# Output projection in 49 products of 128 columns instead of 28 of 256, in a post-norm transformer block on one NeuronCore

## The chip, the cores and the metric

The kernel runs on one core of one Trainium2 chip. The core has a matrix engine (TensorE, "PE"), a vector engine (VectorE, "DVE"), a scalar engine (ScalarE, "ACT"), a general engine (GpSimd, "POOL") and a queue engine (SyncE, "SP") that issues transfers. Each engine takes its instructions in one fixed order, and an instruction waits until what it needs has been signalled by other engines. The metric is the device time of one execution in microseconds (us).

## The reference

Input `x` is 2 sequences (b) of 512 tokens with 512 features, all in float32. The block has two halves:

```
q, k, v = x @ Wq.T, x @ Wk.T, x @ Wv.T        # 32 query heads, 8 key/value heads, 128 wide
q, k    = rmsnorm(q) * qw, rmsnorm(k) * kw
attn    = softmax(q k^T / sqrt(128) + alibi, causal)
x       = layernorm(x + (attn @ v) @ Wo.T)
x       = layernorm(x + ((silu(x @ gate.T * gs) * (x @ up.T * us)) @ down.T) * ds)
```

One group g has one key/value head and its 4 query heads. What the change is about is the output projection `(attn @ v) @ Wo.T`: per group and sequence, 512 tokens by 512 inner features (4 heads of 128) by 512 output features, summed over the 8 groups.

## The kernel before

Work is cut into units (g, b, i): a group, a sequence and a tile of 128 tokens; two neighbouring tiles make a pair. For each pair the kernel projects q, k and v (`project`), normalises and turns them (`heads`), computes scores and softmax tile by tile (`scores`), turns the probabilities and multiplies by v (`attend`), and multiplies the result `aT` by the group's part of Wo (`project_out`). Groups 0 to 5 run over both sequences one after the other; groups 6 and 7 are ordered by sequence, so that the feed-forward half of sequence 0 can start before the attention of sequence 1 is over. Then come the feed-forward part (`ffn_weights`, `ffn_up`, `ffn_down`) and the second normalisation.

**Seven products in place of eight.** The three large matrix products (q/k/v, output, feed-forward) treat their factors as 2 by 2 blocks and form 7 block products in place of 8, by Winograd's form of Strassen's scheme. `seven` (line 619) issues them by the table `PLAN`; the products of sums need four sums of blocks of each factor, which `sums_a` and `sums_b` compute with `tensor` (line 571) on DVE or POOL. For the output projection one product is `depth` = 2 matmuls of 128 by 128 by 256: two token tiles make the rows, two heads each the inner blocks, 256 output features the columns. After each product `accumulate` adds the accumulator bank into `y`, the residual held in the core's memory.

**How a matmul shows.** In float32 one matmul of the program is two records in the trace, each with its own load of weights (LDWEIGHTS) and its own pass over the columns; a transpose is one record. So the 448 output matmuls (8 groups x 2 sequences x 2 pairs x 14) show as 896 records of 128x256 at line 628.

**What sets the order.** All work is entered as operations with a cost, a priority and dependencies, and a planner in `emit` (line 168) places them in time by these costs, chooses DVE, POOL or ACT where several can do an operation, and emits each engine's instructions in the planned order. Buffers come from rings with a number of slots (`Ring`); an operation that needs a slot is planned after the slot's last user. Accumulator banks come from the ring `f` (3 banks) for the large products. Memory is divided into stages: buffers of q/k/v and attention are closed when their last user is placed, and buffers of the feed-forward part open in their place (`close`).

Loads go through SP's queue in planned order; at the start, ACT's queue carries some of them. `load_qkv` loads the group's q, k and v weights from three tensors, `load_o` the group's part of Wo (1 MB), `load_x` the turned input.

Of the kernel before, what the change touches and what calls it, by code (L numbers as in the profile page):

```python
# [10 lines left out]
F32 = mybir.dt.float32  # L11
# [6 lines left out]
P = 128  # L18
# [11 lines left out]
Q = 32  # L30
# [8 lines left out]
MAX_INIT = 3e38  # L39
EARLY = 4  # L40
# [34 lines left out]
class Ring:  # L75

    def __init__(self, name, bufs, shape, dtype=F32, gate=None):
        self.name, self.bufs, self.shape, self.dtype = name, bufs, shape, dtype
        self.gate = gate  # L80
        self.pool = None
        self.slots = [None] * bufs

    def room(self):

        best = None
        for k, b in enumerate(self.slots):
            t = 0.0
            for u in b.users if b else ():
                if u["end"] is None:  # L90
                    break
                t = max(t, u["end"] + LAG[u["eng"]])
            else:
                if best is None or t < best[0]:
                    best = (t, k)
        return best

    def take(self, b):
        k = self.room()[1]
        self.slots[k] = b  # L100
        b.tile = self.pool.tile(self.shape, self.dtype, tag=f"{self.name}{k}", name=b.name, bufs=1)
# [14 lines left out]
class Work:  # L116
# [51 lines left out]
    def emit(self):  # L168
# [23 lines left out]
        def room(o):  # L192

            t = o["at"]
            for b in o["takes"]:
                if b.tile is not None:
                    continue
                r = b.ring
                if r.gate is not None and r.gate["end"] is None:
                    return None  # L200
                found = r.room()
                if found is None:
                    return None
                t = max(t, found[0])
            return t
# [56 lines left out]
def post_ln_block(  # L262
# [4 lines left out]
    wqt: bass.AP,  # L267
    wkt: bass.AP,
    wvt: bass.AP,
# [30 lines left out]
    def ring(stage, name, bufs, shape, dtype=F32, gate=None):  # L300
        r = Ring(name, bufs, shape, dtype, gate)
# [11 lines left out]
    r_y = ring("all", "y", 1, [P, NT, DM])  # L313
    r_xT = ring("all", "xT", 2, [P, NK, S])
    r_sx = ring("all", "sx", 2, [P, 4, 2, S // 2])
    r_gs = ring("all", "gs", 1, [P, NF])
    r_us = ring("all", "us", 1, [P, NF])
    r_ds = ring("all", "ds", 1, [P, DM])
# [4 lines left out]
    r_ms = ring("all", "ms", 3, [P, 2, G + 1])  # L323
    r_inv = ring("all", "inv", 3, [P, 2, G + 1])
# [3 lines left out]
    r_stats = ring("all", "stats", 3, [P, 2, 6])  # L328
# [5 lines left out]
    r_tq = ring("qkv", "tq", 1, [P, 4, 2, W3])  # L334
    r_c = ring("qkv", "c", 2, [P, 2, 2, W3])
    r_sq = ring("qkv", "sq", 2, [P, 2, G + 1, HD])

    r_wo = ring("att", "wo", 2, [P, G, DM])
    r_to = ring("att", "to", 1, [P, 4, 2, WO])
    r_kT = ring("att", "kT", 2, [P, S])  # L340
    r_v = ring("att", "v", 2, [P, NTB, HD])
    r_qT = ring("att", "qT", 6, [P, NQ, G, Q])
    r_bias = ring("att", "bias", 2, [P, S])
    r_prT = ring("att", "prT", 5, [P, S])
    r_aT = ring("att", "aT", 3, [P, 2, G, P])
    r_so = ring("att", "so", 1, [P, 4, 2, P])
    r_rel = ring("att", "rel", 1, [P, S])
    r_vs = ring("att", "vs", 3, [P, HD])
# [8 lines left out]
    y = fixed(r_y, "y")  # L357
    gs_sb, us_sb, ds_sb = fixed(r_gs, "gs_sb"), fixed(r_us, "us_sb"), fixed(r_ds, "ds_sb")
    qw, kw = fixed(r_qw, "qw"), fixed(r_kw, "kw")
    ident, nhalf, rel = fixed(r_id, "ident"), fixed(r_nh, "nhalf"), fixed(r_rel, "rel")  # L360
# [12 lines left out]
    first_pair = {}  # L373
    for p, (g, b, i) in enumerate(pairs):
        first_pair.setdefault(g, p)
# [9 lines left out]
    def load_qkv(g, prio):  # L385
        w = Buf(r_w, f"w_{g}")
        w_qkv[g] = w
        src = wqt[:, ts(g, G * HD)].rearrange("(kc p) (n c) -> p kc n c", p=P, n=2)
        for kc in range(NK):
            at = prio + 0.01 * kc  # L390

            def queries(ns, kc=kc, at=at, queue="SP"):
                load(
                    0.13 * len(ns),
                    at,
                    lambda q: q.dma_start(
                        w[:, kc, ns[0] : ns[-1] + 1, : 2 * HD], src[:, kc, ns[0] : ns[-1] + 1]
                    ),
                    [(w, ("q", n, kc)) for n in ns],
                    queue=queue,  # L400
                )

            def other(n, kc=kc, at=at, queue="ACTQ"):
                load(
                    0.066,
                    at + 0.001,
                    lambda q: q.dma_start(
                        w[:, kc, n, 2 * HD :], (wkt, wvt)[n][ts(kc, P), ts(g, HD)]
                    ),
                    [(w, ("kv", n, kc))],  # L410
                    queue=queue,
                )

            if g == 0 and kc == 0:

                queries((0,))
                load_x(0, kc, 0, at, "ACTQ", 2)
                other(0, queue="SP")
                queries((1,), queue="ACTQ")
                other(1, queue="SP")  # L420
            else:
                queries((0, 1))
                if g == 0:
                    load_x(0, kc, 0, at, "ACTQ")
                    other(0)
                    other(1)
        if g > 0:
            for n, other in enumerate((wkt, wvt)):
                load(
                    0.26,  # L430
                    prio + 0.05,
                    lambda q, n=n, other=other: q.dma_start(
                        w[:, :, n, 2 * HD :],
                        other[:, ts(g, HD)].rearrange("(kc p) c -> p kc c", p=P),
                    ),
                    [(w, ("kv", n, kc)) for kc in range(NK)],
                )

    def load_x(b, kc, q, prio, queue="SP", parts=1):

        n = NTH // parts
        for k in range(parts):
            c0 = q * NTH + k * n
            load(
                0.13 / parts,
                prio + 0.0001 * k,
                lambda e, c0=c0: e.dma_start(
                    xT[b][:, kc, c0 : c0 + n], xt[ts(kc, P), b * S + c0 : b * S + c0 + n]
                ),
                [(xT[b], (kc, c0 // P + m)) for m in range(n // P)],  # L450
# [6 lines left out]
    def w_keys(g, kcs, ns=(0, 1)):  # L457
        w = w_qkv[g]
        return [(w, (k, n, kc)) for k in ("q", "kv") for kc in kcs for n in ns]

    def load_o(g, prio):
        wo = Buf(r_wo, f"wo_{g}")
        w_o[g] = wo
        load(
            1.05,
            prio,
            lambda q: q.dma_start(wo.tile, wot[ts(g, G * HD), :].rearrange("(h p) c -> p h c", p=P)),
            [A(wo)],
        )
# [26 lines left out]
    for b, q in ((0, 1), (1, 0), (1, 1)):  # L496
        for kc in range(NK):
            load_x(b, kc, q, -8.6 + 0.05 * (2 * b + q))
    load_o(0, -8.4)
    load(  # L500
        2.1,
        -8.3,
        lambda q: q.dma_start(y.tile, x.rearrange("(t p) c -> p t c", p=P)),
        [(y, (t, n)) for t in range(NT) for n in range(2)],
    )
# [37 lines left out]
    def make_bias(g, prio):  # L543
        bg = Buf(r_bias, f"bias_{g}")
        bias[g] = bg
        for h in range(G):
# [4 lines left out]
                    bg[ts(h, Q), :], rel[ts(h, Q), :], SLOPES[g * G + h], 1.0, ALU.mult, ALU.mult  # L551
                ),
                [(rel, h)],
# [29 lines left out]
    def sums_a(n, prio, s, a, s_key, a_keys, **kw):  # L583

        add, sub = ALU.add, ALU.subtract
# [3 lines left out]
        tensor(n, prio, g(0), f(1, 0), f(1, 1), add, k(1, 0) + k(1, 1), [s_key(0)], **kw)  # L589
        tensor(n, prio, g(2), f(0, 0), f(1, 0), sub, k(0, 0) + k(1, 0), [s_key(2)], **kw)  # L590
        tensor(n, prio, g(1), g(0), f(0, 0), sub, [s_key(0)] + k(0, 0), [s_key(1)], **kw)
        tensor(n, prio, g(3), f(0, 1), g(1), sub, k(0, 1) + [s_key(1)], [s_key(3)], **kw)

    def sums_b(n, prio, t, b, t_key, b_keys, **kw):

# [1092 lines left out]
```

## Time and profile before

| | |
|---|---|
| median of 3 runs | 1053.89 us (1053.85 to 1054.01) |
| profiled execution, its own time | 1054.3 us |
| its span, first to last instruction | 1052.3 us |
| PE busy | 1043.9 us, 99% |
| DVE, ACT, POOL busy | 633.8, 422.8, 490.0 us |
| granted PE clock | 0.999 |
| PE starts its first real matmul at | 4.39 us |
| last PE record begins at about | 1046 us |

The ends of PE records are modelled: a record of 256 columns is listed with 379 ns although the next one starts some 216 ns later. So the price of a record is read from the distance of starts in the timeline, and not from its listed duration.

### The profile page before, as it was taken

The page shows a single profiled execution, that of the slowest core. Times are in us where ns is not written, and L with a number is a line of the kernel's source. Part 1 is how long each engine was busy: PE and PEld are TensorE (multiplying, and loading weights), DVE is VectorE, ACT ScalarE, POOL GpSimd, SP SyncE. Part 2 cuts the span into 40 slices and gives each one's busy share as a digit, 9 for nine tenths or more (in the row PEclk, how much of TensorE's full clock was granted, in tenths as well). Part 3 has the DMA queues.
Part 4 walks back from the last instruction along what each step waited for, and adds up shares of the span by engine and source line. Part 5 has one row for each costly group of instructions (what it writes and reads, how often), then busy time and mean ns, then how long its engine had stood idle before and what let it go on. Part 6 is the DMA issues. An engine that isn't in the chain of part 4 may idle for free.

```text
span 1052.3 us, 13348 instructions
## 1 busy us (share of the span) xinstructions
PE 1043.9 (99%) x4610; PEld 764.6 (73%) x4610; DVE 633.8 (60%) x1599; ACT 422.8 (40%) x1047; POOL 490.0 (47%) x666
## 2 busy tenths in 40 slices
PE   9999999999999999999999999999999999999997
PEld 5676767676767676767676767676767788888886
DVE  6755565556655565556555656565676477667544
ACT  2543434443434344434444444444454523434100
POOL 6873545454444544454445545454574342114230
PEclk9999999999999999999999999999999999999999
DMA  8310012001100120012001200100101012230011
GB/s 252 119 60 1 1 41 61 1 1 41 60 1 1 40 61 1 1 40 62 1 1 40 61 1 1 40 1 1 40 1 41 21 41 80 76 88 21 1 40 40
DMA packets 44450, 38.93 MB, mean 37 GB/s; under 512 B 3712, under 2 KB 36864, under 8 KB 44384
## 3 DMA queue, kind: packets, MB, share of 16 engines
q1 hardware_dynamic: 42512, 36.92, 11.4%
q10 hardware_dynamic: 1872, 1.18, 0.4%
q8 instruction: 36, 0.59, 0.2%
q14 instruction: 30, 0.25, 0.1%
HBM read 35.99 MB, written 2.10 MB: 36 GB/s over the span
## 4 chain that ended last, share of the span: by engine, by line
PE 99%; DMA 1%; DVE 0%; POOLq 0%; issue 0%; ACT 0%; DVEq 0%
PE pa_q L628 15%; PE sc L958 12%; PE pa L1066 11%; PE pa_o L628 11%; PE pb_q L628 8%; PE pa_h L628 7%; PE pt L1047 6%; PE pb_o L628 5%; PE pc_q L628 4%; PE pb_h L628 4%; PE pa_d L628 3%; PE ptq L905 3%; PE pc_o L628 3%; PE pc_h L628 2%; PE pb_d L628 2%; PE px L1101 2%
## 5 line engine op out<-in xcount | busy, mean ns | idle before, releaser
L983 ACT ACTIVATE pr<-pr,nmax 128x32 f32<-128x32 f32 (+15 forms) x256 | 132.4, 517 | 99.9 <-DVE nmax L967 97.7
L958 PE MATMUL sc<-kT,qT 128*128 128x160 f32 (+15 forms) x512 | 147.9, 403 | 0.0
L1015 POOL TENSOR_SCALAR pr<-pr,rden 128x64 f32<-128x64 f32 (+12 forms) x288 | 135.2, 489 | 12.8 <-DVE rden L998 12.4
L1066 PE MATMUL pa<-prT,v 128*128 128x512 f32 (+1 forms) x320 | 137.0, 510 | 0.0
L967 DVE CUSTOM_DVE_ANT_0 pr<-sc,bias 128x32 f32<-128x32 f32 (+15 forms) x256 | 110.3, 439 | 42.1 <-PE sc L958 39.6
L958 PEld LDWEIGHTS sc<-kT,qT 128*128 128x128 f32 x512 | 88.7, 190 | 53.6 <-issue 29.8
L576 DVE TENSOR_TENSOR y<-y,pa_o 128x256 f32<-128x256 f32 x128 | 53.7, 419 | 95.8 <-PE pa_o L628 95.1
L705 ACT COPY c<-pa_q 128x384 f32<-128x384 f32 x90 | 42.9, 478 | 141.1 <-PE pa_q L628 139.8
L628 PE MATMUL pa_q<-tq,sx 128*128 128x384 f32 x248 | 90.3, 487 | 0.1
L1047 PEld LDWEIGHTS pt<-ident,pr 128*128 128x128 f32 x576 | 69.4, 141 | 28.9 <-issue 15.5
L562 POOL TENSOR_TENSOR inv<-ms,nhalf 128x10 f32<-128x10 f32 (+1 forms) x33 | 63.3, 1919 | 54.9 <-DVE ms L849 53.7
L1047 PE MATMUL pt<-ident,pr 128*128 128x128 f32 x576 | 81.7, 273 | 0.1
L705 ACT COPY prT<-pt 128x512 f32<-128x512 f32 (+1 forms) x92 | 50.3, 549 | 59.2 <-PE pt L1047 59.0
L827 ACT ACTIVATE sq<-c 128x640 f32<-128x640 f32 x64 | 47.2, 738 | 57.7 <-DVE c L576 57.2
L707 DVE COPY prT<-pt 128x512 f32<-128x512 f32 (+1 forms) x68 | 42.1, 627 | 42.7 <-PE pt L1047 42.7
L576 POOL TENSOR_TENSOR sq<-c,inv 128x640 f32<-128x640 f32 x54 | 67.2, 1256 | 0.7
L628 PE MATMUL pa_o<-to,so 128*128 128x256 f32 x256 | 65.7, 379 | 0.0
L707 POOL COPY v<-c 128x128 f32<-128x128 f32 x36 | 10.8, 299 | 116.1 <-DVE c L576 110.5
L1066 PEld LDWEIGHTS pa<-prT,v 128*128 128x128 f32 x320 | 53.4, 191 | 15.1 <-issue 0.5
L576 POOL TENSOR_TENSOR so<-aT 128x256 f32<-128x256 f32 x32 | 22.9, 727 | 87.8 <-PE pb_o L628 72.3
L628 PEld LDWEIGHTS pa_q<-tq,sx 128*128 128x128 f32 x248 | 45.3, 190 | 25.4 <-issue 7.2
L912 ACT ACTIVATE qT<-ptq,qw 128x512 f32<-128x512 f32 x61 | 41.9, 687 | 51.6 <-PE ptq L905 50.8
(161 smaller groups left out, 2085.5 us busy)
## 6 DMA issues: line engine op xcount, KB each, us to landing
wo<-in_wot_dram SPq DMA_DIRECT2D x8, 1024.0 KB, 5.6
w<-in_wqt_dram SPq DMA_DIRECT2D x31, 256.0 KB, 4.1
wi<-in_gwt_dram SPq DMA_DIRECT2D x14, 256.0 KB, 2.8
wi<-in_uwt_dram SPq DMA_DIRECT2D x14, 256.0 KB, 3.2
wdi<-in_dwt_dram SPq DMA_DIRECT2D x10, 256.0 KB, 3.3
y<-in_x_dram SPq DMA_DIRECT2D x1, 2048.0 KB, 12.9
w<-in_wkt_dram SPq DMA_DIRECT2D x7, 256.0 KB, 4.9
w<-in_wvt_dram SPq DMA_DIRECT2D x7, 256.0 KB, 5.2
```

Source lines behind the costliest of these rows:

```text
L562: lambda e: nc.gpsimd.tensor_tensor(dst(), src(), nhalf[:, :n], ALU.pow),
L576: lambda e: vec[e].tensor_tensor(dst(), a(), b(), alu),
L628: nc.tensor.matmul(bank[:rows, :width], lhsT=a(fa, c), rhs=b(fb, c), start=(fresh and c == 0), stop=(c == depth - 1), skip_group_check=True,)
L705: nc.scalar.copy(dst(), src())
L707: vec[e].tensor_copy(dst(), src())
L827: lambda e, r=r: nc.scalar.activation(sq[:, r].rearrange("p h d -> p (h d)"), c(r)[:, : 5 * HD], AF.Square),
L958: lambda e, a=a, w=w, sc=sc: nc.tensor.matmul(sc[:, :w], lhsT=qT[:, a, :, :], rhs=kT[:, :w], start=True, stop=True),
L967: lambda e, a=a, w=w, sc=sc: nc.vector.tensor_tensor_reduce(out=pr[:, a, :w], in0=sc[:, :w], in1=bg[:, S - w :], scale=-1.0, scalar=MAX_IN ...
L983: lambda e, a=a, w=w: nc.scalar.activation(pr[:, a, :w], pr[:, a, :w], AF.Exp, bias=nmax[:, a : a + 1], scale=-1.0, accum_out=den[:, a : a ...
L1015: lambda e, a=a, c0=c0, n=n, to=to, c1=c1: nc.gpsimd.tensor_scalar(to[:, a, c1 : c1 + n], pr[:, a, c0 : c0 + n], rden[:, a : a + 1], 1.0, ...
L1047: nc.tensor.transpose(pt[:, ts(k, P)], pr[:, a, ts(j, P)], ident.tile)
L1066: lambda e, j=j, prT=prT, n=n: nc.tensor.matmul(po[:, S - n :], lhsT=v[:, j, :], rhs=prT[:, :n], start=(j == 0), stop=(j == i), skip_group ...
```

## The change

For groups 0 to 5 (`DEEP` = 6) the output projection of a whole sequence of a group is done at once, with the scheme of seven products at two levels: the outer one on blocks of 256 tokens x 256 inner x 256 output features, the inner one on 128 x 128 x 128. That makes 49 matmuls of 128 by 128 by 128 per group and sequence, where there were 28 of 128 by 128 by 256. The outer products are done in two rounds (four, then three of them); within a round the same inner product of each outer one lies side by side in a bank, so one addition of 128x512 (or 128x384) on DVE takes it away. The sums of outer products are not made in every group: the seven outer products have a cell each in `acc` (two of 7 x 2 x 256 columns), in which they add up over the six groups. Three cells have no place in `y` and start from zero; the four others start as the residual, so that `acc` replaces `y`. After group 5, `gather` combines the seven cells to the four of `y` (14 additions of 128x256 per sequence). Groups 6 and 7 keep one level of seven products, pair by pair (`project_pair`).

More changes come with it:

- `sums_a` and `sums_b` write the first of the four sums over a block that nothing needs afterwards, so rings of sums have 3 slots of a sum instead of 4. Product 5 now uses those blocks. Because weights are overwritten, groups 6 and 7 load their weights once per sequence instead of once.
- Rings change their sizes: `qT` 6 to 3, `sq` 2 to 1, `wo` 2 to 1, `ms`, `inv` and `stats` 3 to 2; in the feed-forward part `wi`, `wf`, `sw` and `gu` from 2 to 1 with a second slot that opens when attention's memory is closed. `vs` goes from 3 to 4.
- The ALiBi bias of a group is made from the bias of the group before, by a ratio of slopes, and the table `rel` has a slot of the bias ring.
- Inputs are laid out with longer rows per transfer: q, k and v weights of a group lie together (rows of 1.5 or 3 KB, one tensor in place of three), `xt` loads four feature chunks in one transfer after the first ones, `wo` and `x` are loaded with rows of 8 and 4 KB. The load of `ds` moves from the start to the feed-forward part.

```diff
-    def project_out(p, prio):
-        g, b, i = pairs[p]
...
-        done, _ = accumulate(t, prio)
-        seven(prio, Factor(a_ap, a_keys), Factor(b_ap, b_keys), P, WO, 2, f"o{p}", done)
+    ROUNDS = (
+        [(2, ("A", 3), ("B", 3)), (4, ("A", 1), ("T", 3)), (1, ("A", 2), ("B", 1)), (5, ("A", 0), ("B", 0))],
+        [(6, ("S", 1), ("T", 1)), (3, ("S", 3), ("B", 2)), (7, ("S", 2), ("T", 2))],
+    )
+    def project_out(g, b, prio):
...
+        sums_a(
+            4 * P,
+            prio,
+            lambda j: so[:, j - 1],
+            lambda r, k: heads_of(1 - r, k),
+            lambda j: (so, j),
+            lambda r, k: keys_of(1 - r),
+        )
+        for number, outer in enumerate(ROUNDS):
+            n = len(outer)
+            si = Buf(r_si, f"si_{g}_{b}_{number}")
...
+            def done(which, bank, c0=c0, n=n):
+                r, k = INTO[which]
...
+                tensor(
+                    n * P,
+                    prio,
+                    cell,
+                    cell,
+                    lambda: bank[:, : n * P].rearrange("p (m c) -> p m c", m=n),
+                    ALU.add,
+                    [A(bank)] + keys,
+                    keys,
+                    ("DVE",),
+                )
+            inner(prio, Factor(a_ap, a_keys), Factor(b_ap, b_keys), n, f"o{g}_{b}_{number}", done)
+    def inner(prio, a, b, n, name, done):
+        banks = {k: Buf(r_f, f"p{k}_{name}") for k in "abc"}
+        last = ()
+        for which, k, fa, fb, fresh in PLAN:
+            bank = banks[k]
+            def mm(e, bank=bank, fa=fa, fb=fb, fresh=fresh):
+                for c in range(n):
+                    nc.tensor.matmul(
+                        bank[:, ts(c, P)],
+                        lhsT=a(fa, c),
+                        rhs=b(fb, c),
+                        start=fresh and c == 0,
+                        stop=True,
+                        skip_group_check=True,
+                    )
...
+            W.add({"PE": n * 0.22}, prio, mm, reads, [A(bank)], last if fresh else ())
...
+            done(which, bank)
+    def gather(b, prio):
+        for r in range(2):
+            for to, what in ((2, 1), (6, 1), (3, 6), (3, 5), (7, 6), (4, 7), (7, 5)):
...
     def sums_o(g, prio, after):
...
+        if g >= DEEP:
+            return
+        ti = t_i[g] = Buf(r_ti, f"ti_{g}")
+        for src, c0, keys in ((w, 0, [(w, m) for m in range(4)]), (t, 4, [(t, j) for j in (1, 2, 3)])):
+            n = len(keys)
+            sums_b(
+                n * P,
+                prio,
+                lambda j, c0=c0, n=n: ti[:, j - 1, c0 : c0 + n, :],
+                lambda r, n, src=src: src[:, :, r, ts(n, P)],
+                lambda j, c0=c0: (ti, (j, c0)),
+                lambda r, n, keys=keys: keys,
+                after=after,
+            )
...
-    r_qT = ring("att", "qT", 6, [P, NQ, G, Q])
+    r_qT = ring("att", "qT", 3, [P, NQ, G, Q])
...
-    r_wi = ring("up", "wi", 2, [P, 2, NK, P], I32, gate_up)
-    r_wf = ring("up", "wf", 2, [P, 2, NK, P], F32, gate_up)
+    r_wi = ring("up", "wi", 1, [P, 2, NK, P], I32)
+    r_wf = ring("up", "wf", 1, [P, 2, NK, P])
...
+    for r in (r_wi, r_wf, r_sw, r_gu):
+        r.add(ring("down", r.name + "b", 1, r.shape, r.dtype))
```

## The prediction

> **What bounds the kernel now.** First the page's busy times and the chain of work that ended last:
>
> ```profile
> PE 1043.9 (99%) x4610; PEld 764.6 (73%) x4610; DVE 633.8 (60%) x1599; ACT 422.8 (40%) x1047; POOL 490.0 (47%) x666
> ...
> PE 99%; DMA 1%; DVE 0%; POOLq 0%; issue 0%; ACT 0%; DVEq 0%
> ```
>
> PE is busy throughout and is the whole chain. A busy PE may still be held up inside, so I next read the waits of PE by what they waited for. All of them:
>
> ```profile
> PE warm L482 <- POOL ident masks.py:199: 1.3, 1, 1.3
> PE pa_h L628 <- ACT gu L705: 0.5, 1, 0.5
> PE pa_q L628 <- DVE c L707: 0.4, 1, 0.4
> PE pp L724 <- DMA w<-in_wkt_dram: 0.2, 1, 0.2
> ```
>
> That is 2.4 us in 1052. So the time is the number of PE records times the price of each; other engines count only where they make PE wait. The price comes from the timeline of PE, from distances of starts (columns: start, duration, engine, line, operation, count):
>
> ```profile
> 500.61 1.03 PE L628 MATMUL pa_o<-to,so 128*128 128x256 f32 x4
> 501.47 1.03 PE L628 MATMUL pb_o<-to,so 128*128 128x256 f32 x4
> 502.33 1.03 PE L628 MATMUL pa_o<-to,so 128*128 128x256 f32 x4
> 503.19 1.04 PE L1047 MATMUL pt<-ident,pr 128*128 128x128 f32 x8
> 504.07 1.03 PE L628 MATMUL pa_o<-to,aT 128*128 128x256 f32 x4
> ```
>
> Four records of 256 columns take 0.86 us, 0.216 each, whether a product or something else follows. Eight transposes of 128 columns take 0.88, about 0.109 each. Half the columns, half the price, if that holds for a matmul.
>
> **The change: the product records.** It is not certain that it holds: a matmul also loads 128x128 float32 weights, and the listed load of a matmul (190 ns) is longer than that of a transpose (141 ns), as the page's groups say. The only 128-column matmuls before are among the scores of the first tiles. Here is PE with its weight loads in the timeline:
>
> ```profile
> 532.31 0.55 PE L958 MATMUL sc<-kT,qT 128*128 128x32 f32 x4
> 532.31 0.41 PEld L958 LDWEIGHTS sc<-kT,qT 128*128 128x128 f32 x3 [0.24 <-issue]
> ...
> 532.65 0.30 PEld L1066 LDWEIGHTS pa<-prT,v 128*128 128x128 f32 x2
> ...
> 533.62 0.61 PE L958 MATMUL sc<-kT,qT 128*128 128x96 f32 x4
> 533.62 0.41 PEld L958 LDWEIGHTS sc<-kT,qT 128*128 128x128 f32 x3 [0.24 <-issue]
> 533.95 0.30 PEld L1066 LDWEIGHTS pa<-prT,v 128*128 128x128 f32 x2
> 534.06 0.59 PE L1066 MATMUL pa<-prT,v 128*128 128x512 f32 x1
> ```
>
> At 532.31 the matmuls have only 32 and 64 columns, so the weight loads set the pace: three starts of loads span 532.31 to 532.65, 0.113 each. At 533.62 (96 and 128 columns) it is 0.11. A load of matmul weights thus takes about 0.112 us and can run beside the matmul before it, and it is slightly longer than the 0.109 of the columns. I take 0.112 per record; it is the nearest row. The bounds are 0.109 (the transposes' pace) and 0.120 (a little is lost at every change of product).
>
> A rule speaks against this. The Trainium skill, page "TensorE: Matmul & The Clock Gate", section "Back-to-back issue gap", says that in a stream of weight loads and matmuls both set the spacing, and gives 81 ns for 128 columns where the columns alone would take 56: 1.45 times. An estimate by that factor: 0.109 x 1.45 = 0.158 us per record, and the new projection would cost 186 us in place of 145. The rows above have precisely such a pair stream at 0.110 to 0.113, in float32; the row decides, and the rule stays as a rival.
>
> Now the count. Before, groups 0 to 5 have 6 x 2 x 2 pairs x 14 matmuls x 2 records = 672 records at 0.216: 145.2 us. After: 6 x 2 x 49 x 2 = 1176 records at 0.112: 131.7 us. **Saved: 13.5 us** (17.0 at 0.109, 4.1 at 0.120). Groups 6 and 7, q/k/v, attention and feed-forward keep their PE records. All this lies on the path, since PE is the path.
>
> **What is added beside PE.** On DVE, 168 additions of a bank of 256 columns at 0.419 (70.4 us) become 84 of 512 columns and 84 of 384. Rows of the same kind of addition from a bank:
>
> ```profile
> L576 DVE TENSOR_TENSOR y<-y,pa_o 128x256 f32<-128x256 f32 x128 | 53.7, 419 | 95.8 <-PE pa_o L628 95.1
> ...
> L576 DVE TENSOR_TENSOR c<-pb_q,c 128x384 f32<-128x384 f32 x62 | 34.4, 554 | 32.7 <-PE pb_q L628 32.6
> ...
> L576 DVE TENSOR_TENSOR y<-y,ps 128x512 f32<-128x512 f32 x8 | 5.5, 685 | 0.9 <-PE ps L1593 0.9
> ```
>
> 84 x 0.685 + 84 x 0.554 = 104 us, so 34 us more. Sums of the left factor were 8 x 256 columns per group and sequence and are now 4 x 512 (outer), 8 x 256 and 4 x 384 (inner): 3,584 more columns, 43,000 over twelve. Inner sums of weights add 4 x 512 + 4 x 384 per group, 21,500. The gathering adds 28 x 256, 7,200. Together 71,700 columns of two-operand work: 96 us if all on DVE (0.685 per 512), 178 us if all on POOL (1.271 per 512, the row of `to` from `wo`). In the built kernel's instruction lists they are mixed, and some old work moves from POOL to DVE; costing every changed row by the durations of its kind, DVE gains 81 us and POOL 60, ACT 22. That makes DVE about 715 us (69%), POOL 550 (53%), ACT 445: all still covered by PE's 1030 us. Fill of `acc` with zeros (3,072 columns, some 2.8 us of DVE before 9 us) lies under the wait for the first weights: DVE idles 2.2 us there now.
>
> **Where a wait could come on PE.** PE's order is fixed, so I looked in it for the distance between a result and its use, counting PE work by the paces above. The first inner product of a round waits for the sums; for round one these can begin when the last part of `aT` is added. From the end of that last attention matmul (`pz`) to the first inner product there lie 10 to 25 us of other PE work in all twelve cases. The chain needs two sums of 512 and four of 256 columns: 2 x 0.685 + 4 x 0.44 = 3.1 us on DVE, 2 x 1.27 + 4 x 0.73 = 5.5 us on POOL. Round two needs the single `si` slot back and four sums of 384: 2.4 to 4 us, against 3.5 to 8 us of other PE work. Tighter is the bank: a product is added away before the next goes on top of it. That addition is 0.27 us longer than now, and the order leaves 0.5 us or more of other work after it. What stands in front on DVE can use this up: the queue behind a late addition holds score maxima, evictions of transposes and so on, all of which PE waits for in turn. Two-operand sums also stretch when both engines work (POOL's `tq` sums have 2577 ns in one group, 1814 in another, same size). Smaller rings (`qT`, `sq`, and the feed-forward's single slots around 840 us) are planned for in the same way. I put **+1.5 us** on all this; 0 to +10 bounds it, since before, the same kind of order lost 0.9 us after the start.
>
> **The start.** The plain first projection is 32 records at 0.323 = 10.3 us, and took 11.5 us (4.39 to 15.89), so late loads cost 1.2. Fewer, longer first transfers can gain at most that; PE cannot begin before 4.39, since its warm-up ends there. Against it: the third product (`pb_q`) now needs sums written over weights and input that the plain products still read, made by POOL at 1.81 a sum after the projection; before, PE waited about 0.3 us at this place. I count 0, with -1.2 to +2. `ds` moves out of the start and to a place with no traffic: nothing. Loads in between are shorter in number and covered by tens of us; `wo` with one slot loads in 5.6 us and has 35 us or more between its last use and the next. The end, 6 us after the last PE record, is unchanged.
>
> **Sum.** Against the profiled execution: 1054.3 - 13.5 + 1.5 + 0 = 1042.3. The median shown is 0.4 lower than that execution, so 1053.9 - 12.0 = **1042 us**.
>
> **Rivals.**
> 1. Full pace: matmuls of 128 columns run at 0.109 as transposes do, nothing waits, the start gains its 1.2: 1053.9 - 17.0 - 1.0 = 1036 us. For it: the difference is 3 ns per record. Against: the loads at 532 us.
> 2. Half eaten: PE waits for additions and sums in many rounds, say 0.3 us in each of 24 rounds; with 0.114 per record (-11) it gives 1053.9 - 11 + 7 = 1050 us. For it: DVE at 69%, more sharing. Against: 2.4 us of waits now, at 60%.
> 3. Slower: DVE's additions become the pace within a round. There a round has 7 products of 0.67 or 0.9 us, one addition each of 0.55 or 0.69. From 13.5 / 168 = 0.08 us per product on, waits outweigh the saving; at 0.15 us per product (25 us) it ends at 1066. Against: each round is mixed with other PE work.
> 4. The spacing rule: 186 - 145 = +41, 1095 us. Against: the rows.
> That the change does not do what it says is excluded for PE's counts: the built instruction list has 588 matmuls of 128x128 and 112 of 128x256 for the output, in place of 448.
>
> **Chances.** Forecast 0.70 (1038 to 1047), rival 1 0.12, rival 2 0.10, rival 3 0.06, rival 4 0.02. A difference under 0.2% (2.1 us) can hardly be told from none; that takes 0.03 out of rival 2. Faster 0.89, same 0.03, slower 0.08. For the range I leave out rivals 3 and 4 and the outer end of the first: 1036 to 1050.
>
> **What would show it.** The records `pa_o` of 128x128 should start 0.112 apart inside a product (right), or 0.109, or 0.12 and more (that step wrong). PE's busy time should fall to about 1032, PE's waits stay under 5 us in all; waits on DVE `acc` additions or on `si` above 10 us would make the forecast wrong, as would a late start of the third product by more than 2 us. DVE should show 700 to 730 us.

## The result and the profile after

The changed kernel takes 1043.28 us (median; 1043.01 to 1043.42), the kernel before beside it 1053.87 us (1053.72 to 1054.01). The ratio is 0.9899 with an interval of 0.9887 to 0.9911: 10.6 us faster. The forecast was 1042.0, with 1036 to 1050 as its range. The profiled execution took 1043.3 us, its span is 1041.5 us, and the granted clock is 0.999 as before.

The page of the changed kernel, busy times and the chain of work that ended last:

```profile
PE 1031.9 (99%) x5114; PEld 768.8 (74%) x5114; DVE 719.0 (69%) x1669; ACT 433.7 (42%) x1097; POOL 567.6 (54%) x724
...
PE 97%; DVE 1%; DMA 1%; POOL 0%; issue 0%; ACT 0%; ACTq 0%; POOLq 0%; DVEq 0%
```

PE has 504 more records (5114 for 4610) and is busy 12.0 us less. It is still the chain, but no longer quite alone in it: 3% of the chain lie on other engines, where it was 1%. The waits of PE by what they waited for (total us, times, longest us):

```profile
PE warm L458 <- POOL ident masks.py:199: 1.3, 1, 1.3
PE pb_q L607 <- DVE c L548: 0.6, 1, 0.6
PE pa_o L607 <- ACT aT L704: 0.5, 1, 0.5
PE pp L723 <- DMA xT<-in_xt_dram: 0.4, 1, 0.4
PE ptq L910 <- DVE sq L548: 0.4, 1, 0.4
PE ptk L932 <- DVE sq L548: 0.3, 1, 0.3
PE pa_q L607 <- ACT c L704: 0.2, 1, 0.2
```

They make 3.7 us, 1.3 more than before. None waits for an addition into `acc`, nor for the sums `si` of the inner products. The price of a record, again from distances of starts in PE's timeline:

```profile
137.11 1.06 PE L1300 MATMUL pa_o<-ti,si 128*128 128x128 f32 x8
138.00 0.60 PE L1052 MATMUL pt<-ident,pr 128*128 128x128 f32 x4
138.44 1.02 PE L1071 MATMUL pa<-prT,v 128*128 128x512 f32 x2
```

Eight records of 128 columns take 0.89 us (137.11 to 138.00), 0.111 each; the four transposes behind them take 0.44, 0.110 each. Over all 1176 records of the two-level projection the mean distance is 0.112 us and the sum 131.7 us, against 145.1 before. The additions on DVE, each shape on its own:

```profile
L548 DVE TENSOR_TENSOR acc<-acc,pa_o 128x512 f32<-128x512 f32 x48 | 32.9, 686 | 17.8 <-PE pa_o L1300 17.1
L548 DVE TENSOR_TENSOR acc<-acc,pa_o 128x384 f32<-128x384 f32 x48 | 26.6, 553 | 23.1 <-PE pa_o L1300 21.8
```

DVE waits for PE before them, and not PE for DVE. From all distances of starts, PE's records add up to 1044.9 us before and 1034.0 after. The 10.9 us between them are 13.4 gained in the projection less 2.5 given back in small delays. The list of waits shows about half of these (its 1.3). Most of them lie at 150 to 200 us (0.9) and at 750 to 850 us (1.6). At 181 us the timeline shows what PE waited for:

```profile
178.80 1.80 POOL L548 TENSOR_TENSOR tq<-w,tq 128x768 f32<-128x768 f32 x1
179.11 2.91 DVE L548 TENSOR_TENSOR sq<-c,inv 128x640 f32<-128x640 f32 x2
```

The first of the two DVE operations ends at 181.29. It took 2.18 us, where the 34 of its kind have a median of 0.82, and POOL's sum stood beside it; `ptq` on PE started at 181.43, 0.57 us later than its pace (0.4 of this is in the list).

### The profile page after: what moved, and what is told of

Its sections match the earlier page's. It is cut to its first block, busy times and chain, and to the rows that moved or that the text cites. A ratio compares the mean times of both kernels' runs of the same rounds, so it can differ in the third digit from the quotient of the medians.

```text
span 1041.5 us, 14505 instructions
## 1 busy us (share of the span) xinstructions
PE 1031.9 (99%) x5114; PEld 768.8 (74%) x5114; DVE 719.0 (69%) x1669; ACT 433.7 (42%) x1097; POOL 567.6 (54%) x724
## 4 chain that ended last, share of the span: by engine, by line
PE 97%; DVE 1%; DMA 1%; POOL 0%; issue 0%; ACT 0%; ACTq 0%; POOLq 0%; DVEq 0%
PE pa_q L607 15%; PE sc L963 12%; PE pa L1071 11%; PE pa_h L607 7%; PE pb_q L607 7%; PE pa_o L1300 7%; PE pt L1052 6%; PE pc_q L607 4%; PE pb_h L607 4%; PE pb_o L1300 4%; PE pa_d L607 3%; PE ptq L910 3%; PE pa_o L607 3%; PE pc_h L607 2%; PE pc_o L1300 2%; PE pb_d L607 2%
## 5 line engine op out<-in xcount | busy, mean ns | idle before, releaser
L1020 POOL TENSOR_SCALAR pr<-pr,rden 128x64 f32<-128x64 f32 (+12 forms) x288 | 151.1, 541 | 39.6 <-DVE rden L1003 36.5
L963 PEld LDWEIGHTS sc<-kT,qT 128*128 128x128 f32 x512 | 86.3, 190 | 40.6 <-issue 17.0
L548 DVE TENSOR_TENSOR acc<-acc,pa_o 128x512 f32<-128x512 f32 (+2 forms) x128 | 72.9, 570 | 57.1 <-PE pa_o L1300 38.9
L704 ACT COPY prT<-pt 128x512 f32<-128x512 f32 (+1 forms) x123 | 65.8, 541 | 96.1 <-PE pt L1052 94.7
L704 ACT COPY gu<-pa_h 128x256 f32<-128x256 f32 (+1 forms) x88 | 32.1, 369 | 77.1 <-PE pa_h L607 62.3
L917 ACT ACTIVATE qT<-ptq,qw 128x512 f32<-128x512 f32 x56 | 38.4, 687 | 44.2 <-PE ptq L910 43.9
L548 DVE TENSOR_TENSOR c<-pb_q,c 128x384 f32<-128x384 f32 x62 | 34.3, 554 | 27.4 <-PE pb_q L607 25.4
L847 DVE TENSOR_REDUCE ms<-sq 128x10 f32<-128x1280 f32 (+1 forms) x33 | 47.5, 1440 | 0.8 <-ACT sq L832 0.7
L988 ACT ACTIVATION_READ_ACCUMULATOR pr<-pr,nmax 128x1 f32 x256 | 48.1, 188 | 0.0
L607 PE MATMUL pb_q<-w,sx 128*128 128x384 f32 x124 | 45.6, 491 | 0.6 <-DVE c L548 0.6
```

What stands on the lines that cost most here:

```text
L548: lambda e: vec[e].tensor_tensor(dst(), a(), b(), alu),
L607: nc.tensor.matmul(bank[:rows, :width], lhsT=a(fa, c), rhs=b(fb, c), start=(fresh and c == 0), stop=(c == depth - 1), skip_group_check=True,)
L704: nc.scalar.copy(dst(), src())
L847: lambda e, cut=cut: nc.vector.tensor_reduce(cut(ms), cut(sq), AX.X, ALU.add),
L963: lambda e, a=a, w=w, sc=sc: nc.tensor.matmul(sc[:, :w], lhsT=qT[:, a, :, :], rhs=kT[:, :w], start=True, stop=True),
L988: lambda e, a=a, w=w: nc.scalar.activation(pr[:, a, :w], pr[:, a, :w], AF.Exp, bias=nmax[:, a : a + 1], scale=-1.0, accum_out=den[:, a : a ...
```

## The experiments

Every run has the kernel before beside it on the same chip (1053.8 to 1054.1 us). Theory: the gain is the price of PE's records, 0.112 us per matmul record of 128 columns, set by the load of its weights; everything else is covered by PE or small. The experiments take it apart: the second level, the price, the additions, and then how far the scheme carries.

**The second level alone.** One level in all eight groups, all other edits kept.

```diff
-DEEP = HKV - 2
+DEEP = 0
```

(The first subtraction among the cells of `acc` in `load_tokens` goes too, since without the second level nothing undoes it.)

> The changed kernel with one level of seven products in all eight groups, all other edits kept (longer rows, sums written over blocks, changed rings). Theory (the second level gives the gain, the rest nothing): the product records cost their 145.2 us again, so 1043.3 + 13.5 = 1056.8 less what the second level cost in waits (up to 2.5), that is 1054 to 1057. Rival (transfers with longer rows and the other edits carry the gain): it stays near 1043 to 1048.

Measured: 1056.4 us (1055.9 to 1057.0), ratio 1.0025 (1.0014 to 1.0036). The second level is worth 13.1 us, close to the 13.4 of the records. The other edits cost about 2.5 us against the kernel before. The changed kernel gives back as much, but not all of it in the same places: with one level PE loses 3.7 us more than before at 750 to 850 us (the changed kernel 1.6), gains 0.7 at the start, and has none of the 0.9 at 150 to 200 us. So PE is late at 750 to 850 us without the second level too; the delay at 150 to 200 us is there only with it.

**The rings.** One suspect for those 2.5 us is the smaller rings. One level again, with `qT` at 6 slots and `sq` at 2 as before; the buffers that only the second level needs make room.

```diff
-    r_sq = ring("qkv", "sq", 1, [P, 2, G + 1, HD])
+    r_sq = ring("qkv", "sq", 2, [P, 2, G + 1, HD])
...
-    r_qT = ring("att", "qT", 3, [P, NQ, G, Q])
+    r_qT = ring("att", "qT", 6, [P, NQ, G, Q])
```

> The kernel with one level in all groups and the other edits kept (1056.4), with the slots of qT and sq put back to 6 and 2; the buffers of the second level's sums, unused there, make the room. Theory (the 2.5 us over the kernel before come from the smaller rings): 1053.9, within 1 us. Rival (they come from sums written over blocks, or from loads): 1056.4 as before.

Measured: 1057.6 us (1057.2 to 1057.8), ratio 1.0035. These two rings are not the cause. With more room the kernel is even 1.2 us slower, so a new order by the planner alone may move the time by about a microsecond, and the 2.5 us may belong to no single edit. Sums written over blocks, the one slot of `wo`, the feed-forward's slots and the new loads remain; which of them costs the 2.5 us stays open.

**The price of a record, without the scheme.** The kernel before, each output matmul of 256 columns cut into two of 128: same columns, twice the records.

```diff
+                cut = P if name[0] == "o" else width
                 for c in range(depth):
-                    nc.tensor.matmul(
-                        bank[:rows, :width],
...
-                        rhs=b(fb, c),
...
+                    for s in range(0, width, cut):
+                        nc.tensor.matmul(
+                            bank[:rows, s : s + cut],
...
+                            rhs=b(fb, c)[:, s : s + cut],
```

> The kernel before, with each output matmul of 256 columns issued as two of 128 into the same bank; nothing else differs. Theory (a record of 128 columns costs 0.112, set by its weight load): 1792 records at 0.112 in place of 896 at 0.216, +7.2 us, 1061. Columns alone (0.109): +1.8, 1055.7. Spacing rule (0.158): +90, 1143.

Measured: 1060.0 us (1059.9 to 1060.3), ratio 1.0059, so +6.2. PE's timeline of this kernel, at the place that the prediction showed of the kernel before:

```profile
503.17 1.05 PE L630 MATMUL pa_o<-to,so 128*128 128x128 f32 x8
504.06 1.06 PE L630 MATMUL pb_o<-to,so 128*128 128x128 f32 x8
504.96 1.06 PE L630 MATMUL pa_o<-to,so 128*128 128x128 f32 x8
505.85 1.04 PE L1049 MATMUL pt<-ident,pr 128*128 128x128 f32 x8
```

A product that took 0.86 us in four records takes 0.89 to 0.90 in eight. The 1792 records sum to 199.9 us where 896 of 256 columns had 193.5: +6.4, which is the whole difference. At the 0.158 of the spacing rule they would be 283 us. The rule falls and 0.112 stands.

**What sets 0.112: columns or weights.** In the four of seven inner products that add onto a bank, only 64 of the 128 moving columns. Half the columns of these products are left out.

```diff
+                m = P if fresh else P // 2
...
-                        bank[:, ts(c, P)],
+                        bank[:, c * P : c * P + m],
...
-                        rhs=b(fb, c),
+                        rhs=b(fb, c)[:, :m],
```

> The changed kernel with 64 columns in place of 128 in the four inner products that do not start a bank (672 of the 1176 records); half of their columns is left out. Theory (weight loads set 0.112): the records keep their pace, 1043 within 1 us. Rival (columns set the pace, 64 at 0.056): 672 x 0.056 = 38 us less, 1005.

Measured: 1041.6 us (1040.7 to 1041.9), only 1.7 less than the changed kernel, although 672 records have half their columns. PE's timeline:

```profile
87.97 1.00 PE L1301 MATMUL pa_o<-ti,si 128*128 128x64 f32 x8
88.81 0.44 PE L1301 MATMUL pc_o<-wo,aT 128*128 128x128 f32 x2
```

Eight records of 64 columns take 0.84 us; the median distance of the 672 is still 112 ns. Only the first record of a run of such records is followed after 56 to 59 ns, as its columns would have it, and the matmuls behind a run mostly give that back (165 ns between the first two full-width records in place of 112). So the load of 128x128 weights is the floor, and the columns lie under it. (That it is not a fixed price of any record shows in the next run, where records with fewer weights fall under it.) A third level of the scheme would buy nothing that way: a product cannot be cheaper than its weights.

**The other side: half the weights.** The same products with 64 weight columns and all 128 moving columns. Half the output rows of these products are left out.

```diff
+                m = P if fresh else P // 2
...
-                        bank[:, ts(c, P)],
-                        lhsT=a(fa, c),
+                        bank[:m, ts(c, P)],
+                        lhsT=a(fa, c)[:, :m],
```

> The changed kernel with 64 columns of weights in place of 128 in the same 672 records, so that half of their output rows is left out; the moving columns stay 128. Theory (the weight load is 3 ns longer than the columns): the records fall to 0.109, 2.0 us less, 1041.3. Rival (0.112 is what a matmul of 128 columns costs, whatever is loaded): 1043.3.

Measured: 1065.5 us (1065.3 to 1065.5): 22 us slower than the changed kernel where 2 us faster were expected. A miss, and an instructive one. PE's timeline, at the same place as in the run before:

```profile
87.52 0.81 PE L963 MATMUL sc<-kT,qT 128*128 128x384 f32 x2
88.25 1.09 PE L1301 MATMUL pa_o<-ti,si 128*64 128x128 f32 x8
89.27 0.49 PE L1301 MATMUL pc_o<-wo,aT 128*128 128x128 f32 x2
89.60 0.39 PE L1301 MATMUL pc_o<-to,aT 128*128 128x128 f32 x2
89.82 0.61 PE L1301 MATMUL pc_o<-wo,aT 128*128 128x128 f32 x4
```

The shape is written rows*columns of the weights. Inside the narrow product the records do stand 0.109 apart, as expected. But the product takes 1.02 us for eight records (0.87 at that pace), and the two full-width records behind it take 0.33 us (89.27 to 89.60) where the next two take 0.22. The single distances show it: 94 ns are lost before the first narrow record, the second comes 160 ns after it, and on the way out the distances are 202 and 214 ns. Over 96 narrow products, 22 us plus the 2 us saved inside them make 0.25 us for each product. Some of the products follow one another directly, so there are 77 trips to 64 columns and back, 0.31 us each. The Trainium skill, page "TensorEngine Tiling (Array Packing)", section "Key Properties", says that a change of tiling mode drains TensorE, with no price; this is what such a change looks like here, if that is what the narrow weights cause. The same signs stand around the 64-row products `px` and `pz` in every kernel of this study (94, 97 and 90 ns lost).

**Are the additions near to being the pace?** Each of the 168 additions of a bank in the six groups is done twice; the products then count double in the output.

```diff
                 )
+                tensor(
+                    n * P,
+                    prio,
+                    cell,
+                    cell,
+                    lambda: bank[:, : n * P].rearrange("p (m c) -> p m c", m=n),
+                    ALU.add,
+                    [A(bank)] + keys,
+                    keys,
+                    ("DVE",),
+                )
```

> The changed kernel with each of the 168 additions of a bank in the two-level projection done twice, one after the other (products count double). DVE gains 84 x 0.685 + 84 x 0.554 = 104 us, 79% busy. Theory (additions lie beside PE with room to spare): +0 to +4 us, 1043 to 1047. Rival (the additions are near the pace of a round, so that they ate the 2.4 us): every product waits for part of its second addition, 168 x 0.2 = 34 us at a third of it, 1060 or more.

Measured: 1054.8 us (1053.8 to 1056.3), 11.5 more than the changed kernel; between the two expectations. DVE's busy time grew by 56 us and not by the 104 of the additions, because the planner moved 31 other operations away from it. The records of the inner products are still 0.113 us apart, so the additions did not become the pace of a round, which is what the rival said. PE waits elsewhere:

```profile
PE pa_q L607 <- ACT c L704: 4.7, 9, 0.6
PE pt L1052 <- POOL pr L1020: 2.9, 2, 2.7
```

The first line could be read as a full ACT; the timeline of two of these nine waits, ACT and PE together, speaks against that:

```profile
289.67 0.48 ACT L704 COPY c<-pa_q 128x384 f32<-128x384 f32 x1 [2.10 <-PE pa_q L607]
290.20 1.56 PE L607 MATMUL pa_q<-tq,sx 128*128 128x384 f32 x4 [0.57 <-ACT c L704]
291.80 0.48 ACT L704 COPY c<-pa_q 128x384 f32<-128x384 f32 x1 [1.65 <-PE pa_q L607]
292.33 1.56 PE L607 MATMUL pa_q<-tq,xT 128*128 128x384 f32 x4 [0.57 <-ACT c L704]
```

ACT itself had waited about 2 us for PE, and PE had nothing between a product and the next use of its bank. So what costs time there is the changed order of PE's own work. The mechanism of the prediction's third rival falls. That the 11.5 us come through the planner's new order is argued from these waits; how much of them a fuller DVE would cost by itself (74% busy in place of 69%) was not told apart.

**One group more with two levels, and two more.**

```diff
-DEEP = HKV - 2
+DEEP = HKV - 1        # seven groups; HKV for all eight
```

> Two levels in seven groups in place of six. Theory: per group and sequence 12.10 - 10.98 = 1.12 us of PE less, two of them: 2.2 us, 1041.0; the gathering moves one group on and is still covered by the last group. Rival (more sums turn into waits): 1043 or more.

> Two levels in all eight groups; the gathering then follows the last group, just ahead of the first normalisation. Theory: 4 x 1.12 = 4.5 us of PE less, 1038.8, if the gathering is covered; for the second sequence little attention is left to cover it, and the 14 additions of at least 0.43 us (6 us) may show: 1039 to 1045. Rival (each two-level projection costs waits): above 1043.

Measured: 1057.3 us (1052.8 to 1057.8) for seven and 1080.6 us (1080.2 to 1081.6) for eight. Both miss: 2.2 and 4.5 us less of PE's records were expected (for eight, up to 6 us more for the gathering), and 14 and 37 us more came. The gathering has moved: its additions start at 616 to 686 us in the changed kernel, and with seven groups at 718 to 748 and 821 to 838 us. Seven groups first; the waits of PE and the stretch that has them (busy us and records of PE, of its weight loads, of DVE, ACT, POOL, then the granted clock, the DMA share and GB/s):

```profile
PE pa_o L607 <- DVE acc L548: 4.1, 2, 3.5
PE pt L1052 <- POOL pr L1020: 3.0, 2, 2.3
PE pa L1071 <- DVE prT L706: 2.9, 1, 2.9
```

```profile
750.00:800.00 50.00, 40.21 (x183) 28.38 (x182) 35.69 (x92) 17.17 (x44) 33.58 (x39) 0.91 0.10 32
```

PE is idle for almost 10 of 50 us, and the granted clock is 0.91. The same view of two stretches, one of which runs past 800 us, shows where the clock fell:

```profile
753.60:757.00 3.40, 3.02 (x6) 2.19 (x7) 2.25 (x8) 1.39 (x4) 3.40 (x8) 0.50 0.00 0
794.60:804.80 10.20, 5.51 (x16) 3.59 (x17) 8.71 (x19) 2.68 (x6) 7.25 (x7) 0.50 0.00 0
```

At half clock a record takes twice its time (below), so of these 8.5 us of PE's work about half, 4.3 us by this estimate, is the clock's share of the 14. The changed kernel and the run without the gathering (below) have the full clock there. The longest wait has an odd cause. The timeline of all engines before it, cut to DVE, POOL and the PE record that waited:

```profile
747.87 5.21 DVE L854 TENSOR_SCALAR ms<-ms 128x10 f32<-128x10 f32 x1
747.94 1.28 POOL L548 TENSOR_TENSOR to<-wo 128x512 f32<-128x512 f32 x1
...
749.17 0.73 POOL L548 TENSOR_TENSOR so<-aT 128x256 f32<-128x256 f32 x1
749.85 1.27 POOL L548 TENSOR_TENSOR wo<-wo 128x512 f32<-128x512 f32 x1
751.07 0.73 POOL L548 TENSOR_TENSOR so<-aT,so 128x256 f32<-128x256 f32 x1
751.75 1.27 POOL L548 TENSOR_TENSOR to<-wo 128x512 f32<-128x512 f32 x1
752.99 0.41 POOL L1020 TENSOR_SCALAR pr<-pr,rden 128x160 f32<-128x160 f32 x1
752.99 0.41 DVE L548 TENSOR_TENSOR acc<-acc,pa_o 128x256 f32<-128x256 f32 x1
...
753.98 2.08 PE L607 MATMUL pa_o<-wo,aT 128*128 128x256 f32 x4 [3.45 <-DVE acc L548]
```

An operation of DVE on 10 columns, which has a median of 174 ns in the changed kernel, stands for 5.21 us. It stands beside five sums of two operands that POOL does without a gap, and ends when POOL turns to a scaling with one tensor. The addition queued behind it on DVE, and with it PE, waits. Then the four records that waited take 1.87 us (753.98 to 755.85) where such four take 0.86. In the changed kernel the longest of these operations is 1.6 us, and four of the 33 are over 0.9; before, the longest was 1.1. The Trainium skill, page "SBUF — State Buffer", section "SBUF: two separate sides", says that DVE in one of its fast modes and GpSimd share a pair of ports as a lock which one instruction holds, the other standing still. This trace goes further: the wait spans five instructions of GpSimd, not one.

With eight groups PE waits 8.1 us for `kT`, 8.0 us for sums of feed-forward weights on DVE, and 3.7 us for the sums `to` of output weights, and three stretches, 27 us together, have half the clock; these were not taken apart.

**Without the gathering.** Seven groups once more, the 28 additions that combine the seven cells left out (so `y` lacks them).

```diff
                 project_out(g, b, u + 2.6)
-                if g == DEEP - 1:
-                    gather(b, u + 2.7)
```

> Two levels in seven groups as in the run before that had this, but the gathering of the seven cells (28 additions of 128x256) is left out, so that the cells are never combined. That run took 1057.3, 14 us more than the changed kernel, with one wait of 3.6 us of a later product on an addition to the cells. Theory A (the gathering in the middle of a sequence's last groups delays the next group's additions): most of the 14 + 2.2 us goes away, 1041 to 1046. Theory B (the sums of weights, which groups 6 and 7 make once per sequence in place of once, crowd DVE and POOL): little changes, 1052 to 1057.

Measured: 1043.9 us (1043.2 to 1044.5). The gathering, with what it crowds together and what waits for it, carries 13.4 of the 14 us. The other finding is that even without it a seventh group gains nothing over six (1043.3): PE's small delays at 750 to 850 us (3.5 us more than in the changed kernel, by distances of starts) take the 2.2 us.

**The held operation, given to another engine.** The scaling of the sums of squares goes from DVE to ACT, with six groups and with seven.

```diff
-                {"DVE": 0.2},
+                {"ACT": 0.2},
...
-                lambda e, cut=cut: nc.vector.tensor_scalar(
-                    cut(ms), cut(ms), 1.0 / HD, RMS_EPS, ALU.mult, ALU.add
+                lambda e, cut=cut: nc.scalar.activation(
+                    cut(ms), cut(ms), AF.Copy, scale=1.0 / HD, bias=RMS_EPS
```

> The changed kernel with one kind of operation, the scaling of the sums of squares before the square root (10 columns, 33 of them, 155 to 1615 ns on VectorE), given to ScalarE instead. Theory: these are held up by GpSimd's sums of two operands, but over six groups only once and by 1.4 us, so little is to be had: 1042 to 1043.5. Rival: ScalarE, which hands the probabilities' exponentials and the copies of banks to TensorE, is the tighter engine in these stretches: 1044 to 1048.

> Seven groups with both levels (1057.3 before), and the scaling of the sums of squares on ScalarE. Theory: the stall of 3.5 us and the slower clock behind it came of that operation standing 5.2 us on VectorE while GpSimd did sums of two operands back to back; without it there, 1042 to 1047, the clock 0.99 or more in 750 to 800 us. Rival: it is the gathering's own additions on VectorE and GpSimd that hold the next group's additions up, whatever stands between them: 1052 or more.

Measured: six groups 1044.7 us (1044.1 to 1045.4), ratio to before 0.9913 (0.9900 to 0.9927); seven groups 1053.2 us (1052.5 to 1054.8), ratio 0.9995 (0.9987 to 1.0004). On ACT the operation takes 197 to 228 ns in all 33 cases, so the holding is gone, and seven groups gain 4.1 us, about the size of the wait that it made. Ten us of the loss are still there, and by distances of starts nine of them lie at 750 to 850 us. The clock at 750 to 800 us is 0.91 again, where 0.99 or more was expected. The waits of PE with seven groups from 740 to 870 us:

```profile
PE sc L963 <- DVE nmax L972: 2.1, 2, 1.0
PE pa_o L607 <- DVE aT L706: 1.1, 1, 1.1
PE ptq L910 <- DVE sq L548: 0.8, 1, 0.8
```

```profile
750.00:800.00 50.00, 45.96 (x202) 31.74 (x201) 36.82 (x99) 22.49 (x59) 27.74 (x40) 0.91 0.10 33
787.90:791.30 3.40, 1.84 (x12) 1.09 (x8) 3.04 (x9) 1.49 (x5) 1.96 (x4) 1.00 0.00 0
791.40:801.60 10.20, 7.82 (x21) 5.11 (x22) 5.74 (x18) 4.80 (x14) 7.96 (x12) 0.50 0.01 2
```

No wait in this list is over 1.1 us, and still the clock fell to one half for 10.2 us, after 3.4 us in which PE was busy for 1.84. By the same estimate as above that is 3.9 of the ten us.

So my theory, which made the held operation the cause of nearly all, was right in kind and wrong in size, and the rival's number (1052 or more) is the one that came. For six groups nothing is gained: 1044.7 lies in the rival's range (ACT tighter), though its interval still touches that of the changed kernel; that ACT is what tightened was not looked into.

**The same, by the planner.** Seven groups, the operation left on DVE, but entered as one that must not lie beside GpSimd's sums.

```diff
                 lambda e, cut=cut: nc.vector.tensor_scalar(
                     cut(ms), cut(ms), 1.0 / HD, RMS_EPS, ALU.mult, ALU.add
...
+                port=True,
```

> Seven groups with both levels, the same scaling left on VectorE but made known to the planner as an operation that must not lie beside GpSimd's sums of two operands, so that it sets them apart. Theory, as of the run with ScalarE: 1042 to 1048, and none of these operations over 0.5 us. Rival: 1052 or more; or, if the planner pushes the operation or GpSimd's sums late, a wait on the one pushed takes the place of the stall, and the time stays between 1048 and 1057.

Measured: 1052.4 us (1050.4 to 1053.7), ratio 0.9987 (0.9980 to 0.9993). No operation of this kind lasts over 0.2 us now, as expected. The time falls by 4.9 us, as with ACT, and a wait takes the place of the stall, as the last rival said. The timeline cut to it:

```profile
773.85 6.25 POOL L1021 TENSOR_SCALAR pr<-pr,rden 128x416 f32<-128x416 f32 x4
...
783.63 0.81 DVE L548 TENSOR_TENSOR sq<-c,inv 128x640 f32<-128x640 f32 x1
...
784.50 0.48 PE L933 MATMUL ptk<-ident,sq 128*128 128x128 f32 x1 [3.77 <-DVE sq L548]
```

Here DVE does 15 sums of two operands one after the other from 773.67 to 783.63, and `sq`, which PE needs, stands behind them. None of the 15 is the gathering's: they are sums of output weights and of feed-forward input. It works the other way round as well: POOL's four scalings of probabilities beside these sums take 6.25 us, 1.48 to 1.64 each, where the 16 of each of these sizes have medians of 0.61 to 0.69. My reading is that the gathering, done just before, pushes other work of DVE and POOL to where PE needs it at once, and that each change of the order only makes another operation late. This is argued from the run without the gathering and not shown step by step. How much of the ten us is the additions' own time and how much the wait of `y` for them was not told apart. No version with the whole result beat the changed kernel.

## Why the prediction was right, point by point

- **Price and count of the records: right, 13.4 us (13.5 predicted).** 1176 records at 0.112 sum to 131.7 us, the number predicted. The reading of the weight loads at 532 us decided this: the runs with split matmuls (0.112, no scheme) and with 64 columns (still 0.112) show that the load of the weights sets it. The ratio of 1.45 that the fourth rival took from the Trainium skill, page "TensorE: Matmul & The Clock Gate", section "Back-to-back issue gap", does not hold for these float32 pairs: 0.112 against the 0.109 of the columns is 1.03.
- **Work beside PE: right.** DVE 719 us (715 predicted), POOL 568 (550), ACT 434 (445). The additions have 0.686 and 0.553 us, as their rows of before said. Doubling them cost 11.5 us where at most 4 were expected, so free time in DVE's share alone is no sure cover.
- **Waits on PE: +1.5 predicted, about +2.5 measured, and only in part for the reasons given.** This is the mis-sized term. The step named the additions into the bank, the sums of the inner products, two-operand sums that stretch when both engines work, and smaller rings. PE waits for neither of the first two, and two of the rings are excluded. The stretching is there: it holds PE at 181 us (0.57 us). The larger part, at 750 to 850 us, comes with one level too, so the second level is not needed for it; from which of the other edits it comes is not known.
- **The start: right.** PE's first product of weights begins at 4.38 us (4.39) and the seven products at 15.91 (15.89), so longer rows moved nothing in this execution, and the third product starts at 18.50 without a wait.
- **Sum.** 1042.3 was predicted for the profiled execution and 1043.3 measured; the 1.0 us is the term of the waits. That the waits came near their size although two of the named causes are absent is in part luck.
- **Rivals.** Full pace (0.109) fell by 3 ns per record, which are the weights'. Half eaten: 2.5 us in place of the 7 it needs. Additions as the pace: not the mechanism even with all of them doubled. The spacing rule: excluded.

## What to carry to other kernels

Where one engine is busy throughout, price a change by distances of starts of its records, and look in the trace for a stretch where the thing that you doubt already sets the pace: two short scores at 532 us told what 1176 new records would cost. A float32 matmul with 128x128 weights is not cheaper than their load (0.112 us here), so cutting columns from 256 to 128 pays almost in full, and cutting half of the products on to 64 brought 1.7 us where 38 would have come if columns set the pace. And where vector work is "covered", ask at which stage it bunches: the same scheme gained 10.6 us with six groups and lost it all with seven, when the combining fell among the last groups, where late results made PE wait and halved its clock.

## What the runs showed of the hardware that was not expected

- Going from weights of 128 columns to weights of 64 and back costs about 0.31 us in the stream of matmuls (202 and 214 ns between records on the way out, for 109 and 112), more than narrow weights save in eight records (3 ns each).
- A DVE operation on 10 columns (median 0.17 us) stood for 5.21 us beside five sums of GpSimd in a row. Given to ACT, it never exceeds 0.23 us.
- After PE had waited 3.45 us, its next records of 256 columns stood about 0.43 us apart in place of 0.216, and the granted clock was 0.50 for 3.4 us. So waits cost more than themselves. A single long wait is not needed: in the run with seven groups and the scaling on ACT, no wait there was over 1.1 us, yet 10.2 us at half clock followed a stretch of 3.4 us with PE busy for 1.84.
